# A graph layer on one core: groups of 512 nodes kept in PSUM against 128-node windows per chunk, with fewer row fetches and other engines for the copies

## The chip, the core and the metric

The kernel runs on one NeuronCore of a Trainium2 chip. The core has a matrix engine (PE; its weight loads are listed apart as PEld), a vector engine (DVE), a scalar engine (ACT), a general engine (POOL, GpSimd) and an engine that only issues transfers (SP). Each engine takes its own instructions strictly in program order and the engines meet through semaphores. DMAs are issued by SP, ACT and POOL; an issue takes its place in the instruction order of the engine that makes it. The metric is the time of the whole program on the device in microseconds (us); smaller is better.

## The reference

Two relational graph layers, then a residual and a normalization, over N = 50,000 nodes of 128 features, 16 relations, 8 basis matrices and E = 850,000 edges sorted by target. 50,000 of the edges are loops from a node to itself; the other M = 800,000 come from other nodes.

```python
def _rgcn_layer(h, src, dst, rel, basis, w_comp, loop_w, bias):
    W = jnp.einsum('rb,bio->rio', w_comp, basis)
    seg = dst.astype(jnp.int32) * N_REL + rel.astype(jnp.int32)
    agg = jax.ops.segment_sum(h[src], seg, num_segments=N_ENT * N_REL)
    agg = agg.reshape(N_ENT, N_REL, -1)
    msg = jnp.einsum('nri,rio->no', agg, W)
    out = msg + h @ loop_w + bias
    return jax.nn.relu(out)
...
x = _layernorm(x + layer(layer(x, ...1), ...2), axis=-1)
```

All arithmetic is float32. Which rows of h an edge needs is known only at run time, so every edge costs the fetch of one 512-byte row.

## The kernel before

A short first part sorts the edge list into a usable form (loops apart, sources in `src`, target offsets in `key`); most of it is spread over the chunks of layer one as the generator `coming`. Then each layer runs over C = 625 chunks. A chunk is K = 10 tiles of 128 edges, 1,280 edges in all, and in target order covers about 80 nodes. A tile's targets are at most WN = 12 neighbouring nodes ("slots"), so a chunk has S = 120 slots.

For chunk c the steps are these:

- Fetch. Ten tiles of 128 rows each are put in one of GATHERS = 5 buffers `rows`. Most tiles come by an indirect DMA on POOL (`gather`, line 204), issued for chunk c + 2 at chunk c. Some come row by row: `row_by_row` loads 128 byte offsets into registers (line 828) and issues 128 DMAs of 512 bytes (line 836), either on SP or on ACT. `HANDS` has SP do one tile in every SP_EVERY = 5 chunks and ACT one in every ACT_EVERY = 5, each tile spread over 5 chunks. That is 248 such tiles a layer (124 for each of the two), 6,002 gathers a layer.
- First product (line 972). PE multiplies each tile with `hot`, a 128 x 96 matrix of basis weights placed at the edge's slot, into `pa`; `ps_a` has two such buffers of five tiles each. DVE copies each full `pa` to `aT` (line 980).
- Second product (`slots`, line 732), two chunks later: `aT` times the eight basis matrices into `ps`, and DVE spreads the 120 slots over J = 4 neighbouring-node columns (line 737).
- To nodes (`to_nodes`, line 768), three chunks later: nodes are kept in groups of GN = 512. A group's sum stays in one PSUM tile of 128 x 512 (`sums`) for all chunks that reach it; `masks_of` builds the masks `own` (line 751).
- Own part of a group (`from_itself`): load of 512 rows `h_own` on SP, transposes (line 695), a copy `hT` on ACT (line 699), products with the basis matrices (line 710), weighting on DVE (line 717) and a reduction (line 725). Weights `lw` for four groups come from `loop_weights` (SP load of `lrel` at line 650, `is_l` on DVE, products at line 670, a copy on ACT at line 678).
- End of a group (`finish`): sum, relu and store on SP (line 793) in layer one; sum, residual, normalization (`normed`) and store (line 798) in layer two. Ends and own parts come once per 512 nodes, 98 groups a layer.

The order on PE, POOL, DVE and ACT is written out by hand (`manual_schedule`): `beside(t, c, ...)` says which step of the own part, the second product and the ends follows tile t of chunk c. In the same loop `next(each)` lets the row fetches go on by a few rows per tile, so row issues, loads and stores stand between each other in SP's queue, and row issues and copies in ACT's. `summed()` is a second way for irregular graphs, which this input does not take.

Of the kernel before, what the change touches and what calls it, by code (L numbers as in the profile page):

```python
# [61 lines left out]
LBITS = 10  # L62
FETCH = 2
# [7 lines left out]
J = 4  # L71
NEAR = 128
SP_EVERY = 5
ACT_EVERY = 5
OFFSETS = 32
# [8 lines left out]
def tile_rgcn_resnorm(  # L84
# [21 lines left out]
    NG = -(-R // P)  # L106
    GN, NGR = J * P, -(-N // (J * P))
    T = P // NR // 2
# [9 lines left out]
    assert D == P and N >= P and edges.shape[0] == 1 and AT * NR == P and PER * NB * WN <= BANK and AT * PER * NB == WEIGHTS and PER == HALF and S <= P and C >= 4 and M > 0 and N % C == 0 and N % J == 0 and J * D == BANK and RUN - LK // 2 == LIVE and 2 * C <= NG * P and N <= 1 << 16 and E % ROW == 0  # L118
# [10 lines left out]
    ROW_AT = dram.tile([2 * C, 2, P], I32, name="ROW_AT")  # L129
    NL = -(-(N + LK) // GN) * GN  # L130
    LREL = dram.tile([2 * NL, 1], I32, name="LREL")

# [66 lines left out]
    ps_o = ctx.enter_context(tc.tile_pool(name="ps_o", bufs=2, space=PSUM))  # L199
    ps_s = ctx.enter_context(tc.tile_pool(name="ps_s", bufs=1, space=PSUM))  # L200
    ps_n = ctx.enter_context(tc.tile_pool(name="ps_n", bufs=2, space=PSUM))
# [6 lines left out]
    def turned(h, m, sb):  # L208

        tp = ps_o.tile([P, BANK], F32, name="po")  # L210
        nc.tensor.transpose(tp[:, :m], h, ident[:m, :m])
        hT = sb.tile([P, P], F32, name="hT")
        nc.scalar.copy(hT[:, :m], tp[:, :m])
        return hT[:, :m]
# [8 lines left out]
    key = consts.tile([P, 2 * C * HALF], U8, name="key")  # L223


    node4 = consts.tile([P, C], F32, name="node4")
    which = consts.tile([P, C, J], U8, name="which")
    col4 = consts.tile([P, P], F32, name="col4")
    nc.gpsimd.iota(col4, pattern=[[J, P]], base=0, channel_multiplier=0, allow_small_or_imprecise_dtypes=True)
    first_of = consts.tile([1, C], F32, name="first_of")  # L230
    apart_by = consts.tile([P, 1], F32, name="apart_by")
# [3 lines left out]
    picked = consts.tile([P, 5 * NG + len(ROWS) + 2], F32, name="picked")  # L235
    ones = consts.tile([P, P], F32, name="ones")
# [9 lines left out]
    nc.vector.tensor_scalar(apart_by, odd, float(NP), None, op0=OP.mult)  # L246
    nc.vector.memset(ones, 1.0)
# [4 lines left out]
    def set_up(pool):  # L252
# [14 lines left out]
        po = ps_o.tile([P, BANK], F32, name="po")  # L267
# [146 lines left out]
    def loops_of(g, pool, m, d_i, k_f, r_i, loop, loops, asked):  # L414
# [14 lines left out]
        nc.vector.scalar_tensor_tensor(to, odd, float(NL), d_i[:, 0:1], op0=OP.mult, op1=OP.add)  # L429
        yield  # L430
        nc.vector.tensor_scalar(picked[0:1, 5 * g + 4 : 5 * g + 5], d_i[0:1, 0:1], float(asked()), None, op0=OP.is_ge)
# [8 lines left out]
    def rows_of(j, pool):  # L440
# [3 lines left out]
        parts = [pool.tile([P, LIVE, 2], F32, name=name) for name in ("full", "parts")]  # L444
        for h in range(2):
            nc.sync.dma_start(
                parts[h][:m],
                FULL[h * NP + r0 * LIVE : h * NP + (r0 + m) * LIVE].rearrange("(p e) w -> p e w", e=LIVE),
            )
        if j:  # L450
            yield
        srcf = pool.tile([P, LIVE], F32, name="both")
        nc.vector.tensor_tensor(srcf[:m], parts[0][:m, :, 0], parts[1][:m, :, 0], op=OP.add)
        node = pool.tile([P, RUN], I32, name="word")[:, :LIVE]
        nc.vector.tensor_tensor(node[:m], parts[0][:m, :, 1], parts[1][:m, :, 1], op=OP.add)
# [3 lines left out]
        def put(of, to):  # L459
# [16 lines left out]

        row_at = pool.tile([P, LIVE], F32, name="real").bitcast(I32)[:, : 2 * P]
        nc.vector.tensor_scalar(
            row_at[:m], srcf[:m, LIVE - 2 * P :], float(N - 1), float(4 * D), op0=OP.min, op1=OP.mult
        )  # L480
        nc.sync.dma_start(ROW_AT[r0 : r0 + m].rearrange("r t e -> r (t e)"), row_at[:m])

# [3 lines left out]
        keyf = pool.tile([P, RUN], I32, name="l_word").bitcast(F32)[:, :LIVE]  # L486
# [6 lines left out]
        if (r0 + m) * LIVE > M:  # L493
# [6 lines left out]
                beyond[:m], place[:m, :LIVE], last[:m], 64.0, op0=OP.is_gt, op1=OP.mult  # L500
# [8 lines left out]
        po = ps_o.tile([P, BANK], F32, name="po")  # L509
# [5 lines left out]
        nc.vector.tensor_copy(first_of[:, c0 : c0 + cs], half[0:1, :, 0])  # L515
        yield
        po = ps_o.tile([P, BANK], F32, name="po")
        for h in range(2):
            nc.tensor.matmul(po[:S, :cs], spread[h], half[:, :, h], start=h == 0, stop=h == 1)
        at_i = pool.tile([P, P // 2], I32, name="at_i")  # L520
        nc.vector.tensor_scalar(at_i[:S, :cs], po[:S, :cs], within[:S], None, op0=OP.add)
        j_i = pool.tile([P, P // 2], I32, name="j_i")
        nc.vector.tensor_scalar(j_i[:S, :cs], at_i[:S, :cs], J - 1, None, op0=OP.bitwise_and)
        yield
        nc.vector.tensor_tensor(node4[:S, c0 : c0 + cs], at_i[:S, :cs], j_i[:S, :cs], op=OP.subtract)
        nc.vector.tensor_tensor(
            which[:S, c0 : c0 + cs, :],
            j_i[:S, :cs, None].to_broadcast([S, cs, J]),
            col[:S, None, :J].to_broadcast([S, cs, J]),
            op=OP.is_equal,  # L530
        )
# [6 lines left out]
            ones[:m, 0:1].to_broadcast([m, LIVE]),  # L538
# [6 lines left out]
    def count_up(pool):  # L545
        last = 5 * NG + len(ROWS)
        off = pool.tile([1, C], F32, name="off_all")
        even = pool.tile([1, C], F32, name="even")
        nc.gpsimd.iota(
            even,  # L550
            pattern=[[N // C, C]],
            base=0,
# [3 lines left out]
        nc.vector.tensor_tensor(off, first_of, even, op=OP.subtract)  # L556
        for i, (most, op) in enumerate(((-NEAR, OP.is_ge), (NEAR, OP.is_le))):
            nc.vector.scalar_tensor_tensor(
                even,
                off,  # L560
                float(most),
                ones[0:1, 0:1].to_broadcast([1, C]),
                op0=op,
                op1=OP.mult,
                accum_out=picked[0:1, last + i : last + i + 1],
            )
# [3 lines left out]
        total = ps_o.tile([P, BANK], F32, name="po")  # L570
# [4 lines left out]
            off[:, 1:2], total[:1, 1:2], float(E + 2 * NG * (P + 1) + 2 * C), None, op0=OP.not_equal  # L575
# [3 lines left out]
    def normed(t, k, m, to, sb):  # L579

        st = sb.tile([P, k, 6], F32, name="st")
        mv = sb.tile([P, k, 2], F32, name="mv")
        for j in range(k):
            nc.vector.bn_stats(st[:m, j, :], t[:, j, :])  # L584
            nc.vector.bn_aggr(mv[:m, j, :], st[:m, j, :])  # L585
        sd = sb.tile([P, k], F32, name="sd")
        nc.scalar.activation(sd[:m], mv[:m, :, 1], AF.Sqrt, bias=eps[:m])  # L587
        yield
        rs = sb.tile([P, k], F32, name="rs")
        nc.vector.reciprocal(rs[:m], sd[:m])  # L590
        nm = sb.tile([P, k], F32, name="nm")
        nc.vector.scalar_tensor_tensor(nm[:m], mv[:m, :, 0], -1.0, rs[:m], op0=OP.mult, op1=OP.mult)
        yield
        for j in range(k):
            nc.scalar.activation(to[:, j, :], t[:, j, :], AF.Identity, bias=nm[:m, j : j + 1], scale=rs[:m, j : j + 1])  # L595

    def chunked():
        with (
# [45 lines left out]
            def loop_weights(g, n):  # L644
# [15 lines left out]
                for h in range(2):  # L660
# [3 lines left out]
                    if h == 0:  # L664
                        yield
# [535 lines left out]
```

## Time and profile before

| what | value |
|---|---|
| median of 3 runs | 22,276.57 us (22,265.25 to 22,299.96) |
| profiled execution | 22,265.25 us, span 22,263.4 us |
| instructions in the span | 293,484 |
| PE, PEld busy | 55%, 41% |
| POOL busy | 51% |
| DVE busy | 37% |
| ACT busy | 2% |
| mean granted PE clock | 0.725 of full speed |
| gathers | 12,004 at 0.95 us on POOL |
| row issues | 31,744 on SP, 31,744 on ACT |

The busy shares leave out the issuing of DMAs and register instructions: ACT's 2% is its copies and activations alone, and SP has no share at all. A line of the waits names the waiting instruction, what it waited for by the profile, the total in us, how often and the longest. In a group of instructions stand line, engine, operation, output and inputs, shape and count, then busy time, mean in ns, and idle time of the engine ahead of it with what ended it. The profile infers who ended a wait from semaphore events; "remote" and "issue" name no producer.

### The profile page before, as it was taken

How to read it: one execution, taken by the hardware profiler on the slowest of the kernel's cores; microseconds unless marked ns; L12 is line 12 of the kernel's file. 1: busy time of each engine (PE TensorE's matmuls, PEld its weight loads, DVE VectorE, ACT ScalarE, POOL GpSimd, SP SyncE). 2: the span in 40 equal slices, each digit the busy share in tenths (PEclk: the TensorE clock that was granted, in tenths of full speed). 3: DMA queues.
4: the chain of work that ended last, by engine and by line, in shares of the span. 5: the costliest groups of instructions: out<-in, count | busy, mean ns of one | idle time of the engine just before them, and what ended most of it. 6: DMA issues, size and time to landing. Idle time of an engine off the chain costs nothing. (4 is left out here: it accounts for less than half of the span.)

```text
span 22263.4 us, 293484 instructions
## 1 busy us (share of the span) xinstructions
PE 12149.2 (55%) x58712; PEld 9182.9 (41%) x58712; DVE 8268.7 (37%) x14006; ACT 421.1 (2%) x896; POOL 11429.7 (51%) x12037
## 2 busy tenths in 40 slices
PE   4555455455555555555555555555555555555555
PEld 3444333343344444444444444443444334444444
DVE  4444334343333333333333333333333333333333
ACT  0000000000000000000000000000000000000000
POOL 4555454445455555555555555555555555555554
PEclk8777777677777777777777777777777777777777
DMA  2111111111111111111111111111111111111111
GB/s 59 52 52 51 47 52 47 46 51 51 46 44 45 43 45 45 45 45 44 45 44 49 47 49 49 49 47 46 48 46 48 47 45 48 48 47 48 47 48 42
DMA packets 654635, 1056.09 MB, mean 47 GB/s; under 512 B 270882, under 2 KB 380438, under 8 KB 652810
## 3 DMA queue, kind: packets, MB, share of 16 engines
q0 software_dynamic: 387680, 794.28, 13.6%
q1 hardware_dynamic: 198426, 225.12, 3.2%
q10 hardware_dynamic: 66704, 17.83, 0.3%
q14 instruction: 1348, 11.04, 0.2%
q8 instruction: 477, 7.82, 0.1%
HBM read 962.55 MB, written 73.59 MB: 47 GB/s over the span
## 5 line engine op out<-in xcount | busy, mean ns | idle before, releaser
L204 POOL DMA_INDIRECT g<-H,src x6002 | 5700.8, 950 | 5180.6 <-PE pa L972 2736.4
L204 POOL DMA_INDIRECT g<-in_x_dram,src x6002 | 5703.0, 950 | 5004.7 <-PE pa L972 2571.4
L972 PE MATMUL pa<-hot,g 128*128 128x96 f32 x24008 | 4840.8, 311 | 2467.4 <-issue 1524.7
L972 PEld LDWEIGHTS pa<-hot,g 128*128 128x128 f32 x24008 | 4404.2, 233 | 4106.9 <-issue 3049.2
L980 DVE COPY aT<-pa 128x480 f32<-128x480 f32 x2500 | 1633.3, 653 | 7334.7 <-remote 3354.2
L710 PE MATMUL po<-basis,hT 128*128 128x512 f32 x3136 | 2108.3, 760 | 3905.3 <-ACT hT L699 2911.9
L732 PE MATMUL ps<-basis,aT 128*120 128x128 f32 x20000 | 3844.4, 318 | 631.9 <-issue 570.4
L732 PEld LDWEIGHTS ps<-basis,aT 128*120 128x120 f32 x20000 | 3127.3, 218 | 727.5 <-issue 652.3
L768 PE MATMUL pn<-slots,own 120*128 120x512 f32 x4128 | 2682.1, 768 | 790.0 <-DVE own L751 537.5
L710 PEld LDWEIGHTS po<-basis,hT 128*128 128x128 f32 x3136 | 573.3, 228 | 4005.1 <-ACT hT L699 2940.7
L717 DVE TENSOR_TENSOR by<-po,lw 128x512 f32<-128x512 f32 x1568 | 1068.7, 686 | 2417.6 <-PE po L710 1851.2
L725 DVE TENSOR_REDUCE ls<-by 128x128 f32<-128x1152 f32 (+1 forms) x784 | 1665.0, 2124 | 34.4
L768 PEld LDWEIGHTS pn<-slots,own 120*128 120x128 f32 x4128 | 896.0, 245 | 1451.4 <-issue 842.6
L890 DVE TENSOR_TENSOR hot<-fixed,own 128x960 f32<-128x960 f32 x1250 | 1446.9, 1158 | 42.9
L737 DVE TENSOR_TENSOR slots<-ps,which 120x512 f32<-120x512 f32 x1250 | 856.1, 685 | 692.9 <-PE pa L972 331.6
L630 DVE TENSOR_SCALAR is_rel<-rel,its_rel 128x640 f32<-128x640 uint8 x314 | 179.9, 573 | 1903.3 <-DMA rel<-REL 1812.9
L670 PE MATMUL po<-each,is_l 64*128 64x32 f32 (+1 forms) x800 | 205.1, 419 | 1074.7 <-DVE is_l L661 1036.7
L670 PEld LDWEIGHTS po<-each,is_l 64*128 64x128 f32 (+1 forms) x800 | 193.2, 324 | 1089.9 <-DVE is_l L661 1049.9
L695 PE MATMUL po<-ident,h_own 128*128 128x128 f32 (+1 forms) x784 | 205.1, 350 | 743.2 <-DMA h_own<-H 544.5
L751 DVE TENSOR_SCALAR own<-col,node 120x128 f32<-120x128 f32 x2064 | 536.5, 302 | 6.5 <-PE pn L768 6.5
L635 PE MATMUL fixed<-each,is_rel 128*128 128x64 f32 x3140 | 471.6, 302 | 74.1 <-issue 67.2
L635 PEld LDWEIGHTS fixed<-each,is_rel 128*128 128x128 f32 x3140 | 454.5, 223 | 74.6 <-issue 65.5
(134 smaller groups left out, 3024.7 us busy)
## 6 DMA issues: line engine op xcount, KB each, us to landing
by_hand<-in_x_dram ACTq DMA_DIRECT2D x15872, 0.5 KB
by_hand<-in_x_dram SPq DMA_DIRECT2D x15872, 0.5 KB
by_hand<-H SPq DMA_DIRECT2D x15872, 0.5 KB
by_hand<-H ACTq DMA_DIRECT2D x15872, 0.5 KB
g<-in_x_dram,src POOLq DMA_INDIRECT x6002
g<-H,src POOLq DMA_INDIRECT x6002
rel<-REL SPq DMA_DIRECT2D x312, 80.0 KB
h_own<-in_x_dram SPq DMA_DIRECT2D x97, 256.0 KB
```

Source lines behind the costliest of these rows:

```text
L204: return nc.gpsimd.indirect_dma_start(out=to, out_offset=None, in_=of, in_offset=bass.IndirectOffsetOnAxis(ap=idx, axis=0))
L635: nc.tensor.matmul(of[:, :, j * NB : (j + 1) * NB], is_rel[:m, j * P : (j + 1) * P], EACH[n][:m], start=True, stop=True,)
L710: nc.tensor.matmul(hb[:m], hT[:, j, :m], BASIS[n][:, b : b + few, :].rearrange("p b d -> p (b d)"), start=True, stop=True,)
L717: nc.vector.tensor_tensor(by[:m, b : b + few, :], hb[:m].rearrange("p (b d) -> p b d", d=D), lw[:m, j, g % T, b : b + few, None].to_broadc ...
L725: nc.vector.tensor_reduce(ls[:m, j, :], by[:m].rearrange("p b d -> p d b"), AX.X, OP.add)
L732: nc.tensor.matmul(ps[: k * WN, :D], aT[:, b, : k * WN], BASIS[n][:, b, :], start=b == 0, stop=b == NB - 1)
L737: nc.vector.tensor_tensor(st[: k * WN], ps[: k * WN, None, :D].to_broadcast([k * WN, J, D]), which[: k * WN, c, :, None].to_broadcast([k * ...
L751: nc.vector.tensor_scalar(own[:k], col4[:k], node4[:k, c : c + 1], float(-g * GN), op0=OP.subtract, op1=OP.is_equal)
L768: nc.tensor.matmul(sums[g], own, of[:k].rearrange("s j d -> s (j d)"), start=c == first(g), stop=c == final(g),)
L890: nc.vector.tensor_tensor(hot[:, : ks(c)], pm[:, c % Q * K : c % Q * K + ks(c), :, None].to_broadcast([P, ks(c), NB, WN]), own[:, : ks(c), ...
L972: nc.tensor.matmul(pa[:, i * NB * WN : (i + 1) * NB * WN], others.get(k + i, g[:, k + i, :]), hot[:, k + i].rearrange("e b w -> e (b w)"), ...
L980: nc.vector.tensor_copy(aT[:, :, k * WN : (k + m) * WN].rearrange("d b (i w) -> d i b w", w=WN), pa[:, : m * NB * WN].rearrange("d (i b w) ...
```

## The change

The short title of the new kernel is "Each gather waits only for the product that read its own tile of the buffer, not the first of each chunk for the last product of the whole buffer", in place of "Groups of 512 nodes; SyncE and ScalarE c". The call that gathers and the buffers it writes are not in the diff. What the diff replaces:

- Row fetches. Each of SP and ACT fetches one tile in BY_HAND = 8 chunks, spread over 8 chunks, 16 registers at a time: 77 tiles each, 154 a layer, and 6,096 gathers a layer.
- Groups. There is no group of 512. A chunk ends in a window of 128 nodes at a base known at run time. Its sum is one PSUM tile of 128 x 128 from two masks (this chunk's slots and the last one's), and windows of neighbouring chunks overlap. SP reads the bases into registers, eight at a time (`at`).
- Own part. It is made per 128 nodes (391 a layer), ahead of the chunk, and its result goes to a DRAM tensor `L[n]`; each chunk loads its window from there (`loaded`), in layer two also its window of x. The window's result is stored for each chunk.
- Engines. ACT, not DVE, copies `aT` from PSUM and `slots` from PSUM. The spreading over four columns goes.
- PSUM. `ps_o` and `ps_n` have one buffer each, the own part's products a pool `ps_h` with two.
- Smaller things: `key` is bf16 and `own` of `hot_of` f32; the first part keeps bases and slots in place of `node4` and `which`; `count_up` checks other bounds.

The core of the diff; removed functions stand above in full.

```diff
-SP_EVERY = 5
-ACT_EVERY = 5
-OFFSETS = 32
+BASES = 8
+BY_HAND = 8
...
+    L = [dram.tile([N, D], F32, name=f"L{n}") for n in range(2)]
...
-    ps_o = ctx.enter_context(tc.tile_pool(name="ps_o", bufs=2, space=PSUM))
-    ps_s = ctx.enter_context(tc.tile_pool(name="ps_s", bufs=1, space=PSUM))
-    ps_n = ctx.enter_context(tc.tile_pool(name="ps_n", bufs=2, space=PSUM))
+    ps_o = ctx.enter_context(tc.tile_pool(name="ps_o", bufs=1, space=PSUM))
+    ps_n = ctx.enter_context(tc.tile_pool(name="ps_n", bufs=1, space=PSUM))
+    ps_h = ctx.enter_context(tc.tile_pool(name="ps_h", bufs=2, space=PSUM))
...
+            def at(c):
+
+                if c % BASES == 0:
+                    _, starts[:] = nc.values_load_multi_w_load_instructions(
+                        base_i[0:1, c : min(C, c + BASES)],
+                        engines=[mybir.EngineType.SP],
...
+                return starts[c % BASES]
...
+            def from_itself(i, of, n, lws):
+
+                m = min(P, N - i * P)
+                if i % AT == 0:
+                    weigh = loop_weights(i, n)
+                    next(weigh)
+                h = sb.tile([P, D], F32, name="h_own")
+                nc.sync.dma_start(h[:m], of[i * P : i * P + m, :])
+                yield
+                if i % AT == 0:
+                    lws[:] = [next(weigh)]
+                lw = lws[0][:, i % AT, :]
+                hT = turned(h[:m], m, sb)
+                yield
...
+                    if b == 0:
+                        po = ps_o.tile([P, D], F32, name="po")
+                        nc.tensor.matmul(po[:m], hT, LOOP[n], start=True, stop=True)
+                        nc.vector.tensor_add(by[:m, NB, :], po[:m], BIAS[n][:m])
                         yield
...
+                ls = sb.tile([P, D], F32, name="ls")
+                nc.vector.tensor_reduce(ls[:m], by[:m].rearrange("p b d -> p d b"), AX.X, OP.add)
+                nc.sync.dma_start(L[n][i * P : i * P + m, :], ls[:m])
                 yield
...
-                nc.vector.tensor_tensor(
-                    st[: k * WN],
-                    ps[: k * WN, None, :D].to_broadcast([k * WN, J, D]),
...
+                st = sb.tile([P, D], F32, name="slots", bufs=5)
+                nc.scalar.copy(st[: k * WN], ps[: k * WN])
                 yield st
...
+                looked = [(c, slot[:, c : c + 1])]
+                if c:
+                    looked.append((c - 1, next_slot[:, c - 1 : c]))
...
+            def nodes_of(c, masks, st, n0, ls, xw, n):
+
+                pn = ps_n.tile([P, D], F32, name="pn")
+                for j, (i, own) in enumerate(masks):
+                    nc.tensor.matmul(pn, own, st[i][: ks(i) * WN], start=j == 0, stop=j == len(masks) - 1)
+                yield
+                a = sb.tile([P, D], F32, name="a")
+                nc.vector.tensor_add(a, pn, ls)
                 if n == 0:
                     yield
+                    h = sb.tile([P, D], F32, name="o")
+                    nc.scalar.activation(h, a, AF.Relu)
+                    nc.sync.dma_start(nodes_at(H1, n0), h.bitcast(U8))
                 else:
+                    nc.vector.scalar_tensor_tensor(a, a, 0.0, xw, op0=OP.max, op1=OP.add)
+                    steps = normed_steps(a, P, sb)
+                    next(steps)
                     yield
+                    nc.sync.dma_start(nodes_at(out, n0), next(steps).bitcast(U8))
                 yield
...
+                few, step = P // BY_HAND, P // BY_HAND // 8
+                for e in range(0, P, few):
...
+                    for i, offset in enumerate(offsets):
+                        if i % step == 0:
+                            yield to
+                        behind[engine] = engine.dma_start(to.bitcast(U8)[e + i : e + i + 1, :], byte[None, ds(offset, 4 * D)]).ins
                     yield to
...
+                def loaded(c):
+
+                    n0 = base[c] = at(c)
+                    ls = sb.tile([P, D], F32, name="ls_of")
+                    nc.sync.dma_start(ls.bitcast(U8), nodes_at(L[n], n0))
...
+                    if n:
+                        xw = sb.tile([P, D], F32, name="xw")
+                        nc.sync.dma_start(xw.bitcast(U8), nodes_at(x, n0))
...
+                def beside(t, c, staged, summing, ending):
+
+                    if t in (0, 5, 6):
+                        next(staged, None)
+                    elif t == 7:
+                        done(staged)
...
+                    if t == 2:
+                        next(ending, None)
+                    elif t == 6:
+                        done(ending)
+                    elif t == 8 and c > 2:
+                        return finish(c - 3)
...
+                    if c > 1:
+                        loaded(c - 2)
...
                             if i == m - 1:
-                                nc.vector.tensor_copy(
+                                nc.scalar.copy(
                                     aT[:, :, k * WN : (k + m) * WN].rearrange("d b (i w) -> d i b w", w=WN),
                                     pa[:, : m * NB * WN].rearrange("d (i b w) -> d i b w", i=m, w=WN),
                                 )
-                            beside(k + i, c, owning, summing)
-                            if k + i < K - 1:
+                            ending = beside(k + i, c, staged, summing, ending)
+                            if k + i < 9:
                                 for each in fetching.values():
                                     next(each, None)
...
+                    for to in [c + 1] if c == 0 else [2, 3] if c == 1 else [c + 2]:
+                        if to < C:
+                            coming_own[to] = [from_itself(i, of, n, lws) for i in own_nodes(to)]
```

An own tile's first step (its load) is taken two chunks ahead, its transposes and `hT` at the start of its chunk, and its products in the chunk after, at tiles 0, 5, 6 and 7. `loaded(c - 2)` is issued at the start of chunk c and used by the ends three chunks behind.

## The prediction

> **What bounds the kernel now.** I read the page's busy shares first, then the waits, then the two queues that issue row fetches, then one stretch of time. The profiled execution took 22,265.25 us (span 22,263.4, 1.9 around it); the median of the three runs is 22,276.57, 11 us above, so I work in the span and add 13 at the end. No busy share explains the span:
>
> ```profile
> PE 12149.2 (55%) x58712; PEld 9182.9 (41%) x58712; DVE 8268.7 (37%) x14006; ACT 421.1 (2%) x896; POOL 11429.7 (51%) x12037
> ```
>
> 1,250 chunks in 22,263 us make 17.8 us each. POOL needs 0.95 + 0.30 us for a gather when it waits for nothing, with 9.6 gathers a chunk 12.0 us. So POOL is held back, and the waits say by whom: by PE, which itself waits for ACT's hT, and ACT is in its row fetches.
>
> ```profile
> POOL g L204 <- PE pa L972: 5307.8, 1890, 31.0
> PE po L710 <- ACT hT L699: 2911.9, 155, 68.0
> ACT hT L699 <- DMA by_hand<-in_x_dram: 4937.2, 84, 116.0
> PE po L670 <- DVE is_l L661: 1036.7, 80, 49.3
> DVE aT L980 <- PE pa L972: 2385.1, 628, 28.3
> DVE aT L980 <- PE ps L732: 701.9, 157, 10.3
> SPq L836 <- DMA by_hand<-in_x_dram: 846.5, 1249, 9.2
> SPq L836 <- DMA by_hand<-H: 773.2, 1208, 4.4
> ```
>
> (Columns: waiter, what it waited for, us in total, times, longest.) See that SP's own waits are small: all rows of its list make about 2.1 ms of 22.3, and still it has nothing left over. The row fetches of line 836, per queue and layer:
>
> ```profile
> L836 ACTq DMA_DIRECT2D by_hand<-in_x_dram x15872: 2/228/1430, 51.7 to 11321.9; - x199
> L836 SPq DMA_DIRECT2D by_hand<-in_x_dram x15872: 2/225/3621, 55.8 to 11357.7; - x199
> L828 SPq TENSOR_LOAD <-row_at x992: 4/2116/4455, 53.2 to 22225.6; - x199
> ```
>
> Undisturbed, one row issue follows the last by 0.325 us; the chain that ended last shows two such steps:
>
> ```profile
> 22197.80 0.23 ACTq L836
> ...
> 22198.12 0.23 ACTq L836
> ```
>
> That is not its usual pace: 31,744 rows in the span are 0.70 us each. The timeline shows why. With POOL idle, ACT issues 73 rows in 37 us (0.51 each, register loads within). When POOL makes its gathers back to back, SP issues 29 rows in 48 us (1.67 each) and ACT 25 in 43:
>
> ```profile
> 5690.08 37.17 ACTq L836 DMA_DIRECT2D by_hand<-in_x_dram  x73
> 5732.11 42.68 ACTq L836 DMA_DIRECT2D by_hand<-in_x_dram  x25
> 5735.50 48.47 SPq L836 DMA_DIRECT2D by_hand<-in_x_dram  x29
> ```
>
> So each gather costs the two issuing queues time. SP's sheet gives the mean: rows 31,744 x 0.325 = 10,317; register loads 992 x 2.116 = 2,099; some 1,500 other issues x 0.37 (the median of the h_own and output rows) = 557; waits 2,100; together 15,070. What is left of the span, 7,190 us over 12,004 gathers, is 0.60 us a gather. SP is full, ACT nearly, and what PE needs through them (lrel, h_own, hT) comes late. PE's stalls then also cost clock: 0.52 granted in the stalled stretch 5700 to 5728, 0.72 in 10000 to 10020.
>
> **The change, part by part.**
>
> Gathers. The gather call and its buffers are not touched; in the trace of before 11,956 semaphore waits of POOL already stand before 12,004 gathers. I cost the new waiting rule at nothing. A row-fetched tile comes 154 times a layer instead of 248, so 6,096 gathers a layer: 188 more in all, 188 x 1.25 = 235 us on POOL, which has the room (it waits 5.3 ms for PE), and 188 x 0.60 = 113 us on each issuing queue, counted below.
>
> SP. Rows 2 x 77 x 128 = 19,712 x 0.325 = 6,406. Register loads: 1,232 of 16 registers; bounds 1.06 us (half) and 2.12 (no shorter), 1.3 taken since the loads are mostly per register: 1,600. Other issues: per chunk an ls_of load and a store of H1 or out (2,500), xw in layer two (625), h_own and the L store per 128 nodes (782 each), rel, lrel, row_at and set-up about 930: 5,600 x 0.37 = 2,078. Bases: 158 register reads, at most 2.1 each, 200 taken. Gathers 12,192 x 0.60 = 7,315. Completion waits in proportion to rows: 1,304. Sum 18.9 ms.
>
> ACT. Rows, loads, gathers and waits as on SP: 6,406 + 1,600 + 7,315 + 1,304 = 16,625. New work in the same queue: 2,500 copies aT from PSUM x 0.583 (the hT row, the nearest in size) = 1,458; 1,250 copies of slots and 782 of hT x 0.265 (the 128x128 lw row) = 538; 625 relu x 0.27 = 169; 625 x (0.297 + 0.482) for sd and the normalized store = 487; lw 26. Sum 2,678, and ACT stands at 19.3 ms: it is the fuller of the two.
>
> DVE. Off go aT 1,633, slots 856, masks 537, the group finish 201, statistics and scalars 208; on come 2,500 masks x 0.302 = 755, additions and relu 1,875 x 0.30 = 563, the bias addition 782 x 0.30 = 235, statistics and scalars 492. From 8.3 to about 6.9 ms, 5.5 us a chunk, hidden below PE and ACT in either kernel; if that cover went it would be a gain of 1.4.
>
> PE. The product to nodes goes from 4,128 records x 0.768 wide to 5,000 x 0.318: 2,682 to 1,590, weight loads 896 to 1,225; the lw products shrink by about 0.1. 0.9 ms less, hidden while PE waits for others. hT and h_own now have a chunk's lead instead of two or three tiles, so the waits for hT (2,912) and is_l (1,037) should mostly go: this is what lets the time come down to the queues' sums at all.
>
> What is late next. aT is now copied by ACT, twice a chunk, with 8 row issues queued between two copies, and behind aT stand PE's next half chunk (two pa buffers) and, through PE, POOL. ACT can no longer run ahead of PE, nor PE of ACT by more than half a chunk. No row shows this wait. Lower bound nothing (a wait can't be negative, and two buffers may cover it); upper bound all idle time that the copying engine, then DVE, had ahead of the same copy:
>
> ```profile
> L980 DVE COPY aT<-pa 128x480 f32<-128x480 f32 x2500 | 1633.3, 653 | 7334.7 <-remote 3354.2 <-PE pa L972 2385.1 <-PE ps L732 701.9
> ```
>
> I take the part in which PE had not yet produced, as ACT meets the same products at the same places: pa 2,385 + ps 702 + pn 322 = 3,409. The "remote" part, with no producer named, I leave out, since the loss to gathers is already in ACT's sheet. SP gets the like: ls_of follows the landing of an L store, and stores follow ACT; 0 to 2.1 us (a register load's round trip) for 782 stores, 0.3 ms taken for what reaches PE.
>
> Start and end: six own tiles are done in a row at chunk 1 and three finishes at the end, under 0.05 ms a layer, left out.
>
> Sum: 19,303 + 3,409 + 300 = 23,012 in the span, 23,025 against the median: 3.4% slower.
>
> The Trainium skill ("DMA: Bandwidth & Descriptors", section "Issuing engines are not separate DMA queues") says that issuing from several engines only saves the sequencer's time to start a DMA, usually small beside the DMA itself. The rows above disagree: 10.3 ms of SP's 22.3 are just that time. By the page the 12,032 issues fewer on each queue would be worth next to nothing, ACT's sum would stay 3.9 ms higher, and the total would come to about 26.9 ms.
>
> **The rivals.**
>
> Faster. The queues are relieved and the handshake is hidden. For it: SP is the full one now and loses 38% of its rows; hT and h_own get their lead; two pa buffers. Against it: at a shorter span gathers stand denser, and in the dense stretch one cost a queue not 0.60 but (48.5 - 29 x 0.325)/29 = 1.3 us. ACT's 19.3 plus 0.14 us more for each of 12,192 gathers: 21.0 ms. It decides where handshake and denser gathers together stay under 22.26 - 19.3 = 3.0 ms, 2.4 us a chunk.
>
> Much slower. The whole idle time of the copying engine comes back on ACT: 19.3 + 7.3 = 26.6 ms at most; midway between this and the forecast 24.8. For it: in burst stretches 8 rows take 13.4 us, more than half a chunk (8.9), so the copy is late just when POOL has buffers to fill. Against it: a late copy holds PE, PE holds POOL, and the burst ends.
>
> No difference: what the queues gain the handshake gives back exactly.
>
> **How the numbers follow.** The forecast's own case, 22.32 to 24.2 ms: 52 in 100. Much slower, above 24.2: 17. Faster: 27, centred on 21.0. No difference: 4. A measurement here can tell about 0.2% from nothing, 45 us. Hence faster 0.27, same 0.04, slower 0.69, and time 23,025. For eight in ten I leave 10 in 100 below 21,100 (about the faster case's centre) and 10 above 25,400 (past the middle of the much slower case).
>
> **What the profile after would show.** Right: ACT idle before aT mostly for PE's pa, PE idle before pa for ACT's aT, almost none for hT and is_l; SP's and ACT's rows 19,712 each; a granted clock near 0.72. Wrong on the handshake, to the fast side: aT's idle time on ACT under 2 ms and PE seldom waiting for aT. Wrong on the queues: SP with large waits of its own for L or stores, ls_of late at the additions. Wrong on gathers: the cost per gather on SP's sheet away from 0.60.

## The result, and the profile after

The changed kernel takes 19,463.47 us (median; 19,438.43 to 19,488.24) against 22,285.60 us for the old one beside it: ratio 0.8734, 95% interval 0.8719 to 0.8749. It is 12.7% faster, where I had forecast 3.4% slower, and the time lies below my range. The profiled execution has a span of 19,470.8 us; the granted PE clock is 0.722, as good as unchanged.

The busy shares of the changed kernel, first:

```profile
PE 11516.4 (59%) x59202; PEld 9701.4 (50%) x59202; DVE 6757.1 (35%) x14585; ACT 2523.1 (13%) x6567; POOL 11559.5 (59%) x12224
```

PE has 0.63 ms less work than before, DVE 1.5 ms less, ACT 2.1 ms more, POOL 0.13 ms more. None of this is the 2.8 ms gained, and no engine's share comes near the span. The waits (waiter, what it waited for, us in total, times, longest):

```profile
ACT aT L972 <- DMA by_hand<-in_x_dram: 2847.3, 569, 46.3
...
POOL g L202 <- PE pa L964: 2632.5, 1711, 21.9
...
PE pa L964 <- ACT aT L972: 1651.6, 555, 20.1
...
ACT aT L972 <- DMA by_hand<-H: 1487.0, 629, 8.1
...
ACT aT L972 <- PE pa L964: 924.0, 258, 12.4
...
PE po L209 <- ACT lw L689: 841.4, 86, 17.3
...
ACT aT L972 <- PE ps L734: 619.3, 181, 15.1
...
PE po L722 <- ACT hT L211: 206.7, 41, 15.6
```

See three things. PE's wait for hT, 2.9 ms before, is 0.2. POOL's wait for PE has halved, from 5.3 to 2.6 ms. And the hand-over that I had feared is there, in both directions: ACT waits for PE ahead of aT (0.92 + 0.62 ms), PE waits for ACT's aT (1.65 ms). Of ACT's idle time ahead of aT, 9.8 ms in all, a larger part stands behind row fetches, 4.3 ms, and 3.4 ms under "remote" and "issue", without a producer:

```profile
L972 ACT COPY aT<-pa 128x480 f32<-128x480 f32 x2500 | 1397.9, 559 | 9783.0 <-DMA by_hand<-in_x_dram 2847.3
```

SP's own waits stay small (all rows of its list together 1.5 ms, before 2.2):

```profile
SPq L727 <- DVE own L864: 261.1, 136, 8.7
SPq L808 <- DMA by_hand<-in_x_dram: 217.5, 382, 3.6
```

So SP is still full: the pauses of over 1.6 us between its instructions, added up from the trace, come to 0.76 ms in 19.5. ACT's come to 5.7 ms (in the old kernel 1.3 on SP and 4.3 on ACT). The instructions of line 808 on SP and the register loads of line 798 (count; duration in ns: least, median, most):

```profile
L808 SPq MOVE by_hand<-in_x_dram x9856: 2/29/1482, 216.6 to 9829.0; - x198
L808 SPq DMA_DIRECT2D by_hand<-in_x_dram x9856: 2/228/1418, 216.6 to 9829.1; - x198
...
L798 SPq TENSOR_LOAD <-row_at x1232: 3/1155/3484, 215.3 to 19434.3; - x176
```

A MOVE (a register instruction; one stands ahead of each row's issue) takes 29 ns, but some take over 1 us. Others are put at 2 ns, so single times are blurred in this trace, and sums say more. In the trace 5,023 of SP's 22,841 MOVEs are longer than 0.1 us. Instructions of 0.6 to 1.0 us on SP number 7,601 (5.4 ms), and steps of 0.65 to 0.75 us between two instructions some 6,440 (4.5 ms): 9.9 ms of SP's 19.5 pass in such pieces of about 0.70 us, which I call stalls below. ACT has only 0.9 ms of them, in the old kernel 3.1 against SP's 8.4. My 0.60 us per gather, 7.2 ms on SP in the old kernel, stood for these; on ACT there is no such term to speak of in the changed kernel.

### The profile page after: what moved, and what is told of

It reads as the page before. It is cut to its first block, busy times and chain, and to the rows that moved or that the text cites. A ratio compares the mean times of both kernels' runs of the same rounds, so it can differ in the third digit from the quotient of the medians.

```text
span 19470.8 us, 266458 instructions
## 1 busy us (share of the span) xinstructions
PE 11516.4 (59%) x59202; PEld 9701.4 (50%) x59202; DVE 6757.1 (35%) x14585; ACT 2523.1 (13%) x6567; POOL 11559.5 (59%) x12224
## 5 line engine op out<-in xcount | busy, mean ns | idle before, releaser
L964 PE MATMUL pa<-hot,g 128*128 128x96 f32 x24384 | 5507.6, 336 | 4909.6 <-issue 3201.8
L964 PEld LDWEIGHTS pa<-hot,g 128*128 128x128 f32 x24384 | 4948.1, 256 | 6503.9 <-issue 4657.1
L734 PEld LDWEIGHTS ps<-basis,aT 128*120 128x120 f32 x20000 | 3525.2, 245 | 292.7 <-issue 271.5
L972 ACT COPY aT<-pa 128x480 f32<-128x480 f32 x2500 | 1397.9, 559 | 9783.0 <-DMA by_hand<-in_x_dram 2847.3
L710 PE MATMUL hb<-basis,hT 128*128 128x512 f32 x3128 | 2411.4, 862 | 59.6 <-issue 52.9
L713 DVE TENSOR_TENSOR by<-hb,lw 128x512 f32<-128x512 f32 x1564 | 1075.4, 688 | 3632.9 <-PE pa L964 941.1
L761 PE MATMUL pn<-slots,own 120*128 120x128 f32 x5000 | 1065.4, 343 | 396.6 <-issue 225.5
L864 DVE TENSOR_TENSOR own<-fixed,key 128x120 f32<-128x120 f32 x1250 | 343.3, 275 | 1346.5 <-PE pa L964 542.0
L710 PEld LDWEIGHTS hb<-basis,hT 128*128 128x128 f32 x3128 | 669.4, 263 | 76.5 <-issue 67.4
L722 PE MATMUL po<-loop,hT 128*128 128x128 f32 x1564 | 399.8, 344 | 419.5 <-issue 210.6
```

Source lines behind the costliest of these rows:

```text
L710: nc.tensor.matmul(hb[:m], hT, BASIS[n][:, b : b + few, :].rearrange("p b d -> p (b d)"), start=True, stop=True)
L713: nc.vector.tensor_tensor(by[:m, b : b + few, :], hb[:m].rearrange("p (b d) -> p b d", d=D), lw[:m, b : b + few, None].to_broadcast([m, fe ...
L722: nc.tensor.matmul(po[:m], hT, LOOP[n], start=True, stop=True)
L734: nc.tensor.matmul(ps[: k * WN], aT[:, b, : k * WN], BASIS[n][:, b, :], start=b == 0, stop=b == NB - 1)
L761: nc.tensor.matmul(pn, own, st[i][: ks(i) * WN], start=j == 0, stop=j == len(masks) - 1)
L964: nc.tensor.matmul(pa[:, i * NB * WN : (i + 1) * NB * WN], g[:, k + i, :] if k + i < ks(c) - by_hand(c) else handed.pop(c), hot[:, k + i]. ...
```

## The experiments

The first four ran on a chip where the old kernel takes 22.50 ms, near the first measurement. The others ran on chips where the same kernel takes 17.41 ms. The difference is a finding of its own (last section); ratios are always to the old kernel on the same chip.

**One part alone: the number of rows (e1, e2, e3).** The old kernel, with one row-fetched tile in 8 chunks on each queue (below: 8/8 rows, in place of 5/5):

```diff
-SP_EVERY = 5
-ACT_EVERY = 5
+SP_EVERY = 8
+ACT_EVERY = 8
```

> The kernel before with SP_EVERY = ACT_EVERY = 8 and nothing else: each queue issues 19,712 rows, as in the changed kernel, and POOL makes 12,192 gathers. Theory Q (the two issuing queues set the time; the changed kernel is faster because of its fewer rows): SP's sheet falls to 6.4 (rows) + 1.3 (loads) + 0.6 (other issues) + 7.3 (gathers) + 1.3 (waits) = 16.9 ms, the waits for hT fall from 2.9 ms to under 1, and the time is 18 to 20 ms. Theory O (the changed kernel is faster because its own part is asked for a chunk ahead, so that PE does not wait for hT, lrel and h_own): the waits stay over 2 ms and the time stays at 21.3 ms or more.

Measured: 19,002.79 us, 0.8445 (0.8426 to 0.8463). The fewer rows alone give more than the whole change; by the two ratios all the rest of the change together costs 0.8734 / 0.8445, 3.4%. Its waits show by which way the rows held the old kernel; before, the first stood at 5,307.8 and the second at 2,911.9:

```profile
POOL g L204 <- PE pa L972: 1661.3, 1727, 22.0
...
PE po L710 <- ACT hT L699: 103.3, 12, 25.8
```

Then each queue alone. With SP_EVERY = 8, ACT_EVERY = 5:

> The kernel before with SP_EVERY = 8 alone (SP 19,712 rows, ACT 31,744). Theory Q with SP as the fuller queue: most of the gain of the run with both at 8, at least two thirds of it; ACT is next at about 20 ms. Theory O: what PE waits for most is hT behind ACT's rows, so SP's rows give at most the is_l and h_own waits, 1 ms: 21.3 ms or more.

Measured: 24,426.88 us, 1.0856 (1.0825 to 1.0886). With SP_EVERY = 5, ACT_EVERY = 8:

> The kernel before with ACT_EVERY = 8 alone (ACT 19,712 rows, SP 31,744). Theory Q with SP as the bound: SP's sheet is unchanged, 22.0 to 22.4 ms, although the waits for hT go. Theory O, as hT's place behind ACT's rows: 2 to 3 ms less, 19.5 to 20.3 ms.

Measured: 22,855.54 us, 1.0157 (1.0129 to 1.0186), where I had expected SP's full queue to keep the time as it was. Both are slower than 5/5 and than 8/8, which none of my theories had: the two queues aren't two sums side by side. The waits of e2, and below them the longest of SP's own:

```profile
POOL g L204 <- PE pa L972: 7294.2, 2028, 49.5
...
PE po L710 <- ACT hT L699: 6072.8, 192, 87.4
ACT hT L699 <- DMA by_hand<-in_x_dram: 5522.2, 91, 120.3
```

```profile
SPq L623 <- DVE own L751: 1193.6, 123, 37.3
```

SP is no longer full (its listed waits are 9.9 ms), it waits for DVE and PE, and ACT's hT, behind ACT's rows, comes later still. One link is in the trace: the DMAs of SP and ACT take their completion semaphores from one ring of eight, and in the old kernel some 8,900 of ACT's 31,744 rows reuse one that SP used last (counted from the first profile's trace). So a row on ACT can wait for a DMA that SP hasn't issued yet, and in the trace of e2 it does: ACT's pauses of over 1.6 us are 8.0 ms, 7.5 of them stand ahead of a DMA whose semaphore SP used last, and in 7.3 SP issued its DMA only after ACT's pause had begun. In e3 it is the other way round: 2.0 of SP's 2.5 ms of pauses stand ahead of a DMA whose semaphore ACT used last. In the changed kernel these are 3.4 of ACT's 5.7 ms, so ACT is in good part held to SP's pace. How much time it would save to give each queue semaphores of its own was not tried.

**Half the rows in the changed kernel (e4).** `BY_HAND = 16` in place of 8.

> The changed kernel with BY_HAND = 16: 76 row-fetched tiles a layer, 9,728 rows on each queue, 12,348 gathers. Theory Q: SP is still the bound in the changed kernel (its waits over the whole span are 1.5 ms of 19.5); with half its rows its sheet falls by 9,984 x 0.325 = 3.2 ms and some 0.6 of register loads and waits to 15.7 ms, and PE, ACT or POOL decide at 16.5 to 18 ms. Theory H (in the changed kernel the copy aT on ACT and PE decide, each waiting for the other, and the queues no longer do): 19.0 to 19.6 ms.

Measured: 18,960.19 us, 0.8425 (0.8407 to 0.8444), between the two theories and nearer the second. Now that both queues have slack, ACT does wait for PE:

```profile
ACT aT L972 <- PE pa L964: 3153.9, 861, 21.4
```

With ps (1.3 ms) that is more than the 3.4 ms that I had added to the time, in a kernel that is 3.5% faster than the changed one. Here the wait stands on an engine with slack: ACT's pauses of over 1.6 us are 12.2 ms. SP's are 6.1 ms in e4 and 3.5 in e1, so SP is no longer full in either; what holds both at 19.0 ms was not settled.

**aT back on DVE, no round trip through L, no rows at all (e5 to e8).** In the old kernel with 8/8 rows and in the changed kernel I exchanged the copying engine; the third kernel leaves the round trip out; the fourth is the old kernel with `by_hand` returning an empty list. The edits of e5 and e7 (e6 has e5's exchange the other way round):

```diff
-                                nc.scalar.copy(
+                                nc.vector.tensor_copy(
...
-                nc.sync.dma_start(L[n][i * P : i * P + m, :], ls[:m])
...
-                    nc.sync.dma_start(ls.bitcast(U8), nodes_at(L[n], n0))
+                    ls = no_ls
```

> The changed kernel with aT copied out of PSUM by VectorE again, as before the change; nothing else differs. ScalarE's queue loses 2,500 copies (1.40 ms of work) and every wait of that copy for TensorE. Theory Q (SyncE's full issue queue is the bound, the wait of ScalarE for TensorE is hidden): 19.2 to 19.7 ms, 0.860 to 0.885 of the time before. Rival P (the prediction's handshake is real and stands in the 19.46 ms, some other term was too large): at least 1.5 ms less, under 18.0 ms, below 0.81. Rival C (the copy on ScalarE is what makes the changed kernel 3.4% longer than the old one with 8/8 rows): 18.7 to 19.1 ms, 0.835 to 0.857.

> The old kernel with one row-fetched tile in 8 chunks per queue (the row share of the change) and aT copied by ScalarE: the second part of the change added to the first. Beside it stands the old kernel with the rows alone, 0.8445. Prediction's handshake at its price (2,500 copies behind row issues, 3.4 ms): 22.4 ms, 0.99. Hidden: within 0.15 ms of the rows alone, 0.838 to 0.852. In between, a copy that costs ScalarE's queue its own 1.4 ms: 0.88 to 0.91.

> The changed kernel without the round trip of the own-node sums through DRAM: the sums are computed but neither stored to L nor loaded as ls_of, and a tile of zeros is added in their place, so the nodes' own messages are left out of the outputs. SyncE loses 2,032 issues (782 stores and 1,250 loads, 0.75 ms at 0.37 us) and the waits ahead of them (0.35 ms). Theory S (these issues on the full SyncE queue are why the changed kernel is 3.4% longer than the old one with 8/8 rows): 18.5 to 19.0 ms, 0.828 to 0.852. Rival (SyncE's queue is full only because it waits for others, so less in it gives nothing): 19.3 to 19.5 ms, 0.866 to 0.876.

> The old kernel with every tile fetched by GpSimd's gathers and no row at all: 496 gathers more than with the old rows (12,500 against 12,004), 39,680 fewer row and load issues in each queue pair. Theory Q (rows are a pure loss at 5/5): GpSimd has 12,500 x 1.25 = 15.6 ms of its own, the rest of the loop as in the old kernel with 8/8 rows: 18.5 to 19.3 ms, 0.825 to 0.858. Rival G (without rows GpSimd is the bound and the rows of 8/8 are worth their place): 19.4 to 20.5 ms, 0.862 to 0.91.

Measured, against 17,411.94: e5 15,416.70 (0.8855), e6 15,421.96 (0.8858), e7 15,408.16 (0.8850), e8 15,799.03 (0.9075). Three different kernels with 12,192 gathers take the same time: 1.264 us a gather. e8 has 12,500 gathers and takes 1.264 each too. Here POOL bounds all four, and nothing on other engines can show, so e5 to e7 decide nothing between the theories that they were made for.

**The same beside the changed kernel (e9, e10, e11), and twice the rows (e12).** e12 has `BY_HAND = 4`.

> The changed kernel itself, as the anchor for the runs beside it. Two kinds of chip have shown so far: one where the old kernel takes 22.3 to 22.5 ms and SyncE spends 8.4 ms in instructions and steps between them of 0.6 to 1.0 us each (9.9 ms in the changed kernel), and one where the old kernel takes 17.4 ms and these are under 0.7 ms in every trace. On the first kind: 0.870 to 0.877 of the old kernel's time. On the second: GpSimd's 12,192 gathers at 1.2645 us back to back, 15.42 ms, 0.883 to 0.888.

> The changed kernel with aT copied by VectorE again, nothing else changed; it stands beside the changed kernel itself on the same chip. On the chip with the stalls, theory Q (SyncE's stalled issue queue is the bound, the wait of ScalarE's copy for TensorE is hidden): within 0.25 ms of the changed kernel. Rival P (the handshake priced in the prediction, 3.4 ms, is really in the time): at least 1.5 ms less. Rival C (the copy is what makes the changed kernel 3.4% longer than the old one with 8/8 rows): 0.4 to 0.8 ms less. On the chip without stalls all three give the gathers' 15.42 ms again.

> The changed kernel without the store and the load of the own-node sums through DRAM (a tile of zeros is added in their place, so the nodes' own messages are left out of the outputs): 2,032 issues less on SyncE. On the chip with the stalls, theory S (SyncE's full queue is why the changed kernel is longer than the old one with 8/8 rows): 2,032 issues at 0.37 us, each with its share of the stalls (9.9 ms over some 27,000 issues and loads, 0.37 us), and 0.35 ms of waits: 1.5 to 1.9 ms off SyncE's sheet, of which the next bound lets 0.4 to 0.9 ms through (the changed kernel with half its rows is 0.5 ms shorter). Rival: SyncE is only waiting for others, and the time stays within 0.1 ms. On the chip without stalls 15.42 ms again.

> The changed kernel with one row-fetched tile per queue in 4 chunks in place of 8: 39,680 rows a queue, 1,240 loads of 32 registers. Theory Q prices each row on the fuller queue at 0.325 us plus the loads and waits in proportion: on the chip with the stalls 19.5 + 6.5 (19,968 rows) + 1.2 (loads) + 1.3 (waits) - 0.2 = 27 to 29 ms, 1.20 to 1.30 of the old kernel. Rival H (the changed kernel is held by the hand-overs between engines and not by its queues): 19.2 to 21 ms. On the chip without stalls SyncE's sheet is 10 ms in the changed kernel, so 10 + 9 = 19 ms at most, 0.89 to 1.09.

Measured, against 17,417.71: e9 15,408.38, 0.8846 (0.8831 to 0.8861); e10 0.8850; e11 0.8847. The gathers bind again; so the gain of the change is about the same on both kinds of chip, but ends at another bound. In e9 the gathers' group of the page has only 0.31 us of idle time ahead of each gather, and in the waits PE now stands behind their landing:

```profile
L202 POOL DMA_INDIRECT g<-in_x_dram,src x6096 | 5804.1, 952 | 1892.0 <-issue 835.2
```

```profile
PE pa L964 <- DMA g<-H,src: 1606.2, 2810, 4.7
```

e12 took 24,774.59 us, 1.4224 (1.4195 to 1.4252): 9.4 ms more for 19,968 rows a queue, 0.47 us each and not 0.325, and that from a time that the gathers hold up; far above my 19 ms. Its waits:

```profile
PE pa L964 <- ACT aT L972: 10839.9, 2065, 24.8
POOL g L202 <- PE pa L964: 10049.6, 4674, 22.2
ACT aT L972 <- DMA by_hand<-in_x_dram: 7862.2, 945, 27.2
```

Here the late copy does hold PE, and PE holds POOL. The copy is late because of the 32 row issues a chunk ahead of it, not because it waits for PE (0.45 ms for pa and ps together). The two queues also hold each other: 4.2 of ACT's 4.4 ms of pauses stand ahead of a DMA whose semaphore SP used last, and 3.9 ms of SP's waits stand ahead of its stores (lines 769 and 775) of what ACT computes. That a row costs more than 0.325 us for this reason is argued, not shown.

**Taking the gathers' cover away (e13, e14), and e12 with aT on DVE (e15), and the old kernel's trace here (e16).** So that POOL no longer sets the time, e13 and e14 have five gathers a chunk, the second half of the products reading the same tiles; e14 copies aT on DVE. The edit of e13:

```diff
-                        for k in range(ks(to) - by_hand(to)):
+                        for k in range(min(PER, ks(to) - by_hand(to))):
...
-                                    g[:, k + i, :] if k + i < ks(c) - by_hand(c) else handed.pop(c),
+                                    g[:, (k + i) % PER, :] if k + i < ks(c) - by_hand(c) else handed.pop(c),
```

> The changed kernel with 5 gathers a chunk in place of 9 or 10; the second half of each chunk's products reads the first half's tiles again, so half of the messages come from wrong sources. 6,250 gathers, 7.9 ms of GpSimd, so that these no longer cover what the queues and the hand-overs take. On the chip without stalls: SyncE's and ScalarE's sheets are 11.5 to 13 ms and TensorE has 11.7 ms of work, so a kernel with a hidden handshake takes 12.5 to 13.8 ms (0.72 to 0.79 of the old kernel); with the handshake uncovered at the prediction's price, 15 ms or more (0.86). On the chip with stalls, theory G (each gather costs the two queues 0.60 to 0.66 us): 19.4 less 5,942 x 0.66, 15.5 ms (0.69); rival (the stalls go with something other than gathers): 18 to 19.5 ms.

> The kernel with half the gathers and, in it, aT copied by VectorE in place of ScalarE: the difference to the run beside it is the price of the handshake on ScalarE where the gathers don't cover it. Rival P (the prediction's 3.4 ms): at least 1.5 ms less than the run beside it. Theory Q (two pa buffers hide it): within 0.25 ms. Between these: the copy's own 1.4 ms on a full ScalarE queue, 0.4 to 1.4 ms less.

> The changed kernel with one row-fetched tile per queue in 4 chunks, and aT copied by VectorE. With the copy on ScalarE this took 24.77 ms (1.42 of the old kernel), TensorE waited 10.8 ms for aT, and the copy waited 10.7 ms behind row issues. Theory R (the rows themselves fill the queues, and the late copy only follows from it): the time falls by no more than the copy's own 1.4 ms, 23.3 to 24.8 ms on the chip without stalls, 1.34 to 1.42. Rival P (with twice the rows the handshake stands in the time, as the prediction had it with the rows as they are): what is left is SyncE's sheet, 39,680 x 0.325 = 12.9, loads 2.5, other issues 2.1, waits 2 to 4: 19.5 to 21.5 ms, 1.12 to 1.24.

> The old kernel itself, for its trace on this chip. On the chip without stalls (17.4 ms; its 12,004 gathers need 15.2): theory Q (the row issues bound it there too) expects SyncE's sheet to fill the span: rows 10.3, loads 2.1, other issues 0.6, the rest waits for DMAs before reuse, 2 to 4 ms, and stalls under 1 ms; GpSimd waits some 2 ms for TensorE, and TensorE's longest waits are for hT and lw as in the first profile. Rival: SyncE has over 3 ms of idle time that waits for TensorE or VectorE, and the order of the own-node work bounds the kernel.

Measured, against 17,411.14: e13 13,383.76, 0.7687 (0.7674 to 0.7700); e14 13,429.85, 0.7714 (0.7701 to 0.7727). Without the gathers' cover the copy on DVE is not faster but 0.3% slower: the hand-over of aT has no price at these rows on this kind of chip. SP is full in e13 (pauses of over 1.6 us: 0.59 ms), so its queue about fills these 13.4 ms. The waits of e13 and, below them, of e14:

```profile
PE pa L964 <- ACT aT L972: 2519.8, 1317, 11.3
```

```profile
PE ps L734 <- ACT slots L739: 1372.8, 605, 10.0
```

In e14 ACT's next copy, slots, takes over as what PE waits for. So the exchange tests the aT hand-over, not all of ACT's. e15, at 23,956.49 us, 1.3757 (1.3729 to 1.3784), shows the same more strongly: 0.8 ms less than e12, within the copy's own 1.4, and PE waits for the other copy.

```profile
PE ps L734 <- ACT slots L739: 8426.5, 1061, 27.6
```

With twice the rows any small copy in ACT's queue is late; which one hardly matters. Whether both copies on DVE would help e12 was not tried.

e16, the old kernel here, has one time, 17,395.98 us, with a span of 17,394.2. The MOVEs of its line 836, and below them those of the first profile of the same kernel (span 22,263.4 us):

```profile
L836 SPq MOVE by_hand<-in_x_dram x15872: 29/29/42, 55.8 to 8756.6; - x199
```

```profile
L836 SPq MOVE by_hand<-in_x_dram x15872: 2/29/1409, 55.7 to 11357.6; - x199
```

Not one MOVE on SP is longer than 42 ns there; in the first profile 5,285 of 31,748 are over 100. SP is full all the same (pauses of over 1.6 us: 1.5 ms). The waits of ACT and PE, and below them SP's own, which are for earlier rows and longer than in the first profile (there 847 and 773 us):

```profile
ACT hT L699 <- DMA by_hand<-in_x_dram: 3915.1, 90, 67.4
...
PE po L710 <- ACT hT L699: 3078.5, 189, 42.5
```

```profile
SPq L836 <- DMA by_hand<-in_x_dram: 1565.7, 2824, 8.9
SPq L836 <- DMA by_hand<-H: 1495.2, 2906, 8.3
```

So the rows hold the old kernel back on both kinds of chip (e8, which has none, takes 15.80 ms here against 17.41), and the waits show the same way: rows ahead of hT on ACT, hT ahead of PE.

**What the rest of the change costs (e17, e18).** e17 is e13 without the round trip through L; e18 is the old kernel with 8/8 rows and five gathers a chunk.

> The changed kernel with half its gathers, and also without the store to L and the load of ls_of (zeros are added in their place): half of the messages come from wrong sources and the nodes' own messages are left out. With half the gathers alone it took 13.38 ms (0.769 of the old kernel) on the chip without stalls, and SyncE had only 0.55 ms of pauses over 1.6 us in it. Theory S (SyncE's issue queue is that kernel's bound, and the changed kernel's extra issues are what it pays): 2,032 issues at 0.37 us are 0.75 ms, with 0.6 ms of waits ahead of them: 12.0 to 12.8 ms, 0.69 to 0.735. Rival (SyncE is full only by waiting on others): 13.2 to 13.4 ms, 0.76 to 0.77. On a chip with stalls the same difference, in proportion, from an unknown start.

> The old kernel with one row-fetched tile in 8 chunks per queue and 5 gathers a chunk (half of the messages come from wrong sources): the row share of the change alone, without the cover of the gathers, against the whole change at 0.769. Theory S: SyncE has rows 19,712 x 0.40 = 7.9, loads 616 x 2.14 = 1.3, other issues 0.6, waits 2: 11.8 ms, and TensorE with 10 to 11 ms of work is next: 11.5 to 12.8 ms, 0.66 to 0.735, so that the rest of the change costs 0.6 to 1.9 ms of queue time. Rival (the rest of the change costs nothing, its own-node order is worth as much as its issues cost): 13.1 to 13.7 ms, 0.75 to 0.79.

Measured, against 17,416.42: e17 12,839.71, 0.7371 (0.7359 to 0.7383), just outside the expected interval: 0.54 ms for 2,032 issues, 0.27 us each. e18 11,656.51, 0.6691 (0.6679 to 0.6702). With equal rows and equal gathers the old order is 1.7 ms shorter than the changed kernel's 13.38 ms. A third of the difference is the round trip through L on SP's queue, shown by e17; the rest (the per-chunk loads, stores and copies on the two queues) is argued from their count. In e18 SP has 1.5 ms of pauses again, and PE is the busiest:

```profile
PE 9764.0 (84%) x58712; PEld 7641.7 (66%) x58712; DVE 8146.7 (70%) x14006; ACT 421.8 (4%) x896; POOL 5953.2 (51%) x6283
```

Two simple versions beat both kernels where the stalls are: the old kernel with 8/8 rows (e1, 0.8445) and the changed one with half its rows (e4, 0.8425). On the other chips the old kernel with 8/8 rows and the copy on ACT (e6, 0.8858) is level with the changed kernel (0.8846), both at the gathers' bound.

## Why the prediction was wrong

**The step that failed** is the handshake term: 3,409 us for ACT waiting for PE ahead of aT, and 300 us of SP's ties, added to ACT's sheet of 19,303. Without them the sum is 19.3 ms on ACT and 18.9 on SP; the span is 19.47. The wait itself was foreseen rightly in kind, but it is 1.5 ms for pa and ps, where I took 3.1. In its place the runs showed that it lies in slack: ACT has 5.7 ms of pauses, and e13 against e14 prices the aT hand-over at nothing. e4 has 3.2 ms of it for pa alone, and is faster. The exchange of e13 and e14 ran on a chip without stalls; for the chip of the forecast the pauses and e4 speak, and the exchange itself is missing there.

**What made me add it** is the statement that ACT is "the fuller of the two". I charged ACT 0.60 us a gather as on SP, 7,315 us. In the trace of before ACT has 3.1 ms of stalls to SP's 8.4; after, 0.9 to 9.9. With the stalls at 0.9 in place of 7.3 ACT's sheet is some 12.9 ms (the span less ACT's pauses is 13.8), and 3.4 ms more on it change nothing. Already in the first profile ACT had 4.3 ms of pauses to SP's 1.3; and ACT's sum and SP's are not independent, as the shared semaphores show. That its 19.3 ms hit the time was chance; SP's sheet is the one that binds.

**SP's sheet.** Rows 6,406 (the count as forecast, at 0.325 us); loads 1,232 x 1.155 = 1,423 (1,600 taken); other issues 2,078 as worked out; waits 1,494 (1,304); bases 200. What is left of the 19,471 is 7,870, 0.645 us for each of 12,192 gathers (0.60). Forecast 18.9, measured 19.5: right to 3%. But the split is wrong. In e16 the old kernel's SP queue is full without stalls at 17.39 ms, where my undisturbed terms made 15.07, 2.3 ms too little. The row's price is right there (the step from one row issue to the next is 0.324 us in the median); the waits are 4.0 ms in place of 2.1. The gathers' term, 7.2 ms, was too large: the two chips differ by 4.9 ms, 0.41 us a gather. That the sum held all the same is partly luck: the stalls grew from 8.4 to 9.9 ms while the gathers hardly changed in number.

**Gathers.** 188 more, 12,192, as forecast. That a gather costs the queues time can hold only on the chip with stalls: in e9 they run back to back at 1.264 us, and no MOVE on SP is over 42 ns. No run there had fewer gathers and the same rows, so the price of a gather was not shown apart.

**The small sizes** were right: aT on ACT 0.559 us (0.583 taken), hT 0.270 (0.265), DVE 6.76 ms (6.9), hT's wait gone. PE lost 0.63 ms (0.9).

**The rivals.** "Faster" names the right mechanism, queues relieved and handshake hidden, with 21.0 ms; its price for denser gathers, 0.14 us more each, was too high: 0.045. It had 27 in 100. What I should have weighed is e1's question: the change of the rows alone, 12,032 issues fewer on each of the two queues, without anything of the rest. Its answer, 15.6%, would have put the sign beyond doubt, and the rest of the change would have been a loss of 3.4% on top.

**The rule that was weighed.** The Trainium skill ("DMA: Bandwidth & Descriptors", section "Issuing engines are not separate DMA queues") calls the time to initiate a DMA usually small beside the DMA itself. The runs disagree for 512-byte rows: e1 only has 24,064 of them come by 188 gathers in place of single issues on SP and ACT, and the time falls by 15.6%.

## What to carry to other kernels

Before a wait is added to a sum, ask whether its engine is the one that is full: sum up each queue's own pauses from the trace, for each queue apart, and don't carry a cost measured on one queue over to another. When a change bundles many parts, price first, by itself, the part that relieves the full queue, since here it gave 15.6% and the rest took 3.4% back. In queues that mix long runs of small DMA issues with short copies, the copy's lateness grows with the issues ahead of it: on the chips without stalls it was free at 16 row issues a chunk and went with 9.4 ms more at 32. Where two queues share completion semaphores, look whether the pauses of one stand ahead of DMAs whose semaphore the other used last, before either is lightened alone.

## What the hardware showed that was not expected

- The same kernel took 22.3 to 22.5 ms on some chips and 17.4 ms on others, with a granted clock of 0.725 and 0.779. Where it took 22.3 ms, MOVEs of SP that need 29 ns took up to 1.4 us, and 8.4 ms passed in pieces of about 0.70 us; where it took 17.4, no MOVE took over 42 ns, and such pieces make 0.3 ms. The chips differ by 4.9 ms in the old kernel, so not all of the 8.4 is lost time. In the first profile the pieces go with dense gathers: 10-us stretches with under 2 us of gathers hold 0.6 us of such pieces on SP, those with 6 us or more hold 5.0. In e9 the gathers are denser still, and the pieces make 0.6 ms. What causes them stays open.
- Lightening one of two issuing queues made the kernel slower, by 8.6% (SP) and 1.6% (ACT); lightening both made it 15.6% faster. SP's and ACT's DMAs share eight completion semaphores in turn, which ties one queue's progress to the other's: in the run with SP lightened, 7.5 of ACT's 8.0 ms of pauses stand ahead of a DMA whose semaphore SP used last. How much of the loss would go with separate semaphores was not measured.
- A register load of 16 values takes 1.16 us on SP (changed kernel, median), one of 32 takes 2.12 (old kernel).
